# Seven products for the output projections of even blocks, and one whole turn for the reciprocals of the softmax sums

## The chip, the cores and the metric

One NeuronCore of one Trainium2 chip runs the whole kernel. The metric is the device time of one execution in microseconds (us). Engines are named as in the profile: PE is TensorE, DVE is VectorE, ACT is ScalarE, POOL is GpSimd, and SP is SyncE, whose queue issues almost all DMAs.

## The reference, cut to what matters

A transformer block with conditioned norms (adaLN), float32 throughout. B = 8 sequences of T = 1024 tokens, D = 512 channels, H = 16 heads of 32, hidden size HD = 2048:

```python
mod = silu(condition) @ Wada + bada                      # six rows of D per sequence
sh_a, sc_a, gt_a, sh_m, sc_m, gt_m = split(mod, 6, axis=1)
xm = layernorm(x, g1, be1) * (1 + sc_a) + sh_a
x = x + gt_a * (causal_attention(xm, Wqkv) @ Wproj + bproj)
xm = layernorm(x, g2, be2) * (1 + sc_m) + sh_m
x = x + gt_m * (gelu(xm @ W1 + b1) @ W2 + b2)
```

The change touches the product with Wproj, and the reciprocal of the row sums by which the softmax divides.

## The kernel before, in words

**Blocks.** The 8 x 1024 tokens are 16 blocks of 512 (`blocks`, L90): two halves per sequence. An even block n attends to its own 512 keys, an odd one to those and to the 512 of the block before it, so odd blocks have the longer attention. For each block the kernel computes k, q and v from the first norm, attends, projects the result with Wproj (`proj`), adds it to the residual, norms it a second time (key `m{n}`, steps `mt`), and runs the MLP: four `u` steps (up) and four `d` parts (down).

**Seven products.** Nearly every 512 x 512 x 512 product is made by a Strassen scheme (`strassen`, L896): quarters of 256, seven products instead of eight, each with a moving operand of 256 columns. `ORDER` (L304) lists the seven weight pieces. Sums of weight quarters (S1 to S4) are made once and kept in DRAM; sums of the activation's quarters (T1 to T4) are made anew each time by DVE and POOL. Three partial results stay in SBUF between the products: `p1`, `u2` and `u4`, one buffer each in the pool `tmp`. The last two products of a call go on as a side thread (`tail`, L975) while the main thread walks on; a later call that still finds the previous tail unfinished (`tail_key`) waits with `u2` for it (L960). The down parts `d` use the same three buffers: `u1` and `u3` in `p1`, `u5` in `u4`, `u2` in `u2` (L1364), and hold `u2` and `u5` from one part to the next.

**Output projections.** `by_quarters` (L292) chooses how block n is projected. Odd blocks 1 to 13 go through `project_quarters` (L1067), which calls `strassen` with `settled`, a function that gates each quarter of the result and adds it to the residual. The T sums live in the tiles of the second norm (`xm_m`, `t_m`), which are allocated early for that in `sums_of` (L1089). Blocks 0, the even ones and 15 go the direct way (`project_out`, L1131): four tiles of 128 tokens, each an accumulation over four pieces of Wproj with a moving operand of 512 columns, a DVE instruction that multiplies PSUM with the gate into `y` (L208), and one addition to the residual `xr` by POOL or DVE (L170 or L167, whichever `either` thinks will be done first).

**What sets the order.** The instruction order on each engine is written by the program itself. `plan` (L246) lists the linear steps of each window w; in window w the core attends block w, while the linear stream does the projection, second norm and MLP of block w - 1 and the k, q, v of block w + 1. A cost model (`now`, `written`, `left`, `note_*`) stands for each engine's clock; `work` advances the linear thread with the shortest wait, and `step_aside` and `pace` interleave it with attention units. In odd windows from w = 5 on the order is: d parts 1 and 2 of block w - 2, `proj` of the even block n = w - 1, `mt` of n, d part 3 of block w - 2, k and q of w + 1, then the `u` steps of n (L269). So `proj` of an even block stands between two d parts which share `u2` and `u4`.

**From the projection to the MLP.** After `proj` come row statistics (DVE L623, L624), the power for 1/sqrt (POOL L645 to L648), the normalized rows `hat_m` (L659, L664), their turn by 32 x 32 blocks (DVE L704) and through DRAM (DMAs L713, L718), the modulation (L775, L781) and the T sums (L791 to L796). Only then can the first `u` step run.

**Activation tiles.** `xm` and `t` have two buffers each and are handed out in turn: one to the first norms (`a{n}`), one to the second norms (`m{n}`), because allocations of the two kinds alternate.

**Weights.** Pieces of 256 KB go through a ring of 8 (`fetch`, L351) in a fixed order; a piece is loaded when the piece eight places ahead of it is released.

**Reciprocals.** `finish` (L1820) ends a head group g of block n. A matmul with ones gives the row sums, already repeated over 32 partitions; ACT copies them to `rec` and the numerator to `top`. `gather` turns a quarter of `rec` (128 columns) by 32 x 32 blocks into a small tile `squares` (L1850) and takes the reciprocals of the 4 columns that matter (L1852); there are four such jobs. `spread_out` (L1857) turns the 16 reciprocals back over 512 columns, and one multiplication makes the result in `qT` (L1885).

Matmuls on 128 x 32 tiles are issued four at a time, once per strip of 32 columns, and each float32 matmul stands in the trace as two instructions. So one call of `matmul` (L212) is 8 instructions; it is called a set below.

Of the kernel before, what the change touches and what calls it, by code (L numbers as in the profile page):

```python
# [22 lines left out]
def kernel(  # L23
# [268 lines left out]
    def by_quarters(n):  # L292
        return 0 < n < NB - 1 and (blocks[n][1])

# [192 lines left out]
    def norm_columns(name, shift_at, gain_at, o_g, o_b):  # L487

        gain = const.tile([P, NC, B], F32, tag=f"gain{name}", name=f"gain{name}")
        shift = const.tile([P, NC, B], F32, tag=f"shift{name}", name=f"shift{name}")  # L490
        one_plus = small.tile([P, NC, B], F32, tag="onep", name=f"onep{name}", bufs=1)
        nc.vector.tensor_scalar(one_plus, modT[:, ts(gain_at, NC), :], 1.0, None, ALU.add)
# [232 lines left out]
    def modulated(key, gain, shift, b, guards):  # L725
# [170 lines left out]
    def strassen(step, x, dest, target, row, done, settled=None):  # L896
# [52 lines left out]

        k1, k2, k4 = "p1", "u2", "u4"  # L950
        a = yield from product("A11", "B11")
# [33 lines left out]
        written[key] = NEVER  # L985
        tail_key[0] = key
        start(tail())
# [79 lines left out]
    def project_quarters(n):  # L1067
# [752 lines left out]
    def finish(n, g):  # L1820
# [24 lines left out]
        part = TB // 4  # L1845
        wide = TB // 4

        def gather(i):
            squares = small.tile([P, wide], F32, tag="squares", name=f"squares_{n}_{g}_{i}", bufs=1)
            nc.vector.transpose(squares, rec[:, ts(i, wide)])  # L1850
            some = inverse[:, ts(i, wide // Q)]
            nc.vector.reciprocal(some, squares.rearrange("p (a i) -> p a i", i=Q)[:, :, 0])  # L1852
            note("DVE", 160 + 1.05 * wide + 100, [kr], [kr])

        def spread_out(i=0, m=TB):
            some = inverse[:, i * m // Q : (i + 1) * m // Q].unsqueeze(2).to_broadcast([P, m // Q, Q])
            nc.vector.transpose(rec[:, ts(i, m)].rearrange("p (a i) -> p a i", i=Q), some)  # L1857
            note("DVE", 140 + 1.05 * m, [kr], [kr])

        inverse = small.tile([P, TB // Q], F32, tag="inverse", name=f"inverse_{n}_{g}", bufs=1)  # L1860
        if (n, g) == groups[-1]:
            for i in range(NTT):
                gather(i)
                spread_out(i, part)
# [5 lines left out]
        if (n, g) == first_end:  # L1870
            for i in range(4):
                gather(i)
            spread_out()
# [15 lines left out]

        for i in range(4):  # L1890
            add_job(lambda i=i: gather(i), [kr], g == NC - 1)
        add_job(quotient, [kr], g == NC - 1)
# [115 lines left out]
    for n in range(NB):  # L2008
# [80 lines left out]
```

## Time and profile before

| | us |
|---|---|
| median of 3 runs (lowest, highest) | 3508.98 (3507.87, 3513.93) |
| the profiled execution's own time | 3501.11 |
| its span, first to last instruction | 3499.4 |
| PE busy | 3441.3 |
| DVE busy | 2203.8 |
| POOL busy | 2113.7 |
| ACT busy | 1212.8 |

The profiled execution's own time is 1.7 us above its span. A share of busy time is an average over stages; the groups of instructions (by line, engine and shape) give the count, the busy time and the mean duration of one, and after the bar the idle time of that engine just before them. The clock that PE was granted was 0.998 of full speed over the span.

### The profile page before, as it was taken

How to read it: one execution, taken by the hardware profiler on the slowest of the kernel's cores; microseconds unless marked ns; L12 is line 12 of the kernel's file. 1: busy time of each engine (PE TensorE's matmuls, PEld its weight loads, DVE VectorE, ACT ScalarE, POOL GpSimd, SP SyncE). 2: the span in 40 equal slices, each digit the busy share in tenths (PEclk: the TensorE clock that was granted, in tenths of full speed). 3: DMA queues.
4: the chain of work that ended last, by engine and by line, in shares of the span. 5: the costliest groups of instructions: out<-in, count | busy, mean ns of one | idle time of the engine just before them, and what ended most of it. 6: DMA issues, size and time to landing. Idle time of an engine off the chain costs nothing. (4 is left out here: it accounts for less than half of the span.)

```text
span 3499.4 us, 122173 instructions
## 1 busy us (share of the span) xinstructions
PE 3441.3 (98%) x55101; PEld 1750.9 (50%) x55101; DVE 2203.8 (63%) x2808; ACT 1212.8 (35%) x1272; POOL 2113.7 (60%) x2255
## 2 busy tenths in 40 slices
PE   8999999999999999999999999999999999999999
PEld 4444455445544555445554455544555445554555
DVE  5775675565666566565666656665666656656573
ACT  2335333342343513335232442333423333323521
POOL 3667847667366663767627676375762857628640
PEclk9999999999999999999999999999999999999999
DMA  6763444535535455363554535545455454543344
GB/s 213 237 188 104 137 125 139 147 104 171 147 118 158 119 162 149 103 182 116 152 152 127 159 116 152 153 137 146 130 154 143 130 144 132 154 126 98 104 134 140
DMA packets 335580, 498.84 MB, mean 143 GB/s; under 512 B 27724, under 2 KB 184460, under 8 KB 331476
## 3 DMA queue, kind: packets, MB, share of 16 engines
q1 hardware_dynamic: 334944, 490.99, 47.8%
q8 instruction: 434, 7.11, 0.8%
q14 instruction: 86, 0.70, 0.1%
q10 hardware_dynamic: 116, 0.03, 0.0%
HBM read 432.13 MB, written 56.69 MB: 140 GB/s over the span
## 5 line engine op out<-in xcount | busy, mean ns | idle before, releaser
L1911 POOL TENSOR_TENSOR pT<-pT,pT 128x256 f32<-128x256 f32 (+3 forms) x1254 | 1224.7, 1012 | 238.9 <-PE po L1810 123.9
L1782 ACT ACTIVATE pT<-st 128x2048 f32<-128x2048 f32 x288 | 541.1, 1879 | 1017.5 <-PE st L1770 886.3
L217 PE MATMUL bank<-w,hT 128*32 128x256 f32 x14336 | 822.1, 380 | 0.0
L1694 DVE TENSOR_REDUCE mx<-sc 128x4 f32<-128x2048 f32 (+3 forms) x383 | 663.3, 1753 | 200.5 <-PE sc L1679 194.7
L217 PEld LDWEIGHTS bank<-w,hT 128*32 128x32 f32 x14336 | 448.0, 110 | 389.8 <-issue 109.7
L217 PE MATMUL bank<-xm_m,w 128*32 128x256 f32 x8192 | 497.4, 381 | 2.3 <-ACT p_u L197 1.0
L217 PE MATMUL bank<-t_m,w 128*32 128x256 f32 x6144 | 384.0, 380 | 2.5 <-DVE qT L208 1.4
L217 PEld LDWEIGHTS bank<-xm_m,w 128*32 128x32 f32 x8192 | 255.5, 110 | 227.3 <-issue 56.6
L1787 POOL TENSOR_SCALAR_AFFINE_SELECT pT<-pT 128x512 f32<-128x512 f32 x256 | 177.3, 710 | 313.7 <-ACT pT L1782 313.3
L1679 PE MATMUL sc<-kT,qT 32*128 32x512 f32 (+3 forms) x3064 | 328.0, 520 | 3.1 <-DVE mx L1694 1.8
L1691 DVE TENSOR_TENSOR sc<-sc,mask 128x1024 f32<-128x1024 f32 (+1 forms) x160 | 162.8, 1017 | 255.2 <-PE sc L1679 210.8
L1810 PE MATMUL po<-pT,v 128*32 128x512 f32 (+3 forms) x3048 | 301.7, 490 | 2.5 <-POOL pT L1787 2.3
L1770 PE MATMUL st<-qT,kT 32*128 32x512 f32 (+3 forms) x3072 | 302.7, 487 | 0.0
L217 PEld LDWEIGHTS bank<-t_m,w 128*32 128x32 f32 x6144 | 188.9, 110 | 178.8 <-issue 49.8
L217 PE MATMUL bank<-xm_a,w 128*32 128x256 f32 x3968 | 241.6, 380 | 2.4 <-ACT p_k L197 1.1
L1679 PEld LDWEIGHTS sc<-kT,qT 32*128 32x128 f32 x3064 | 129.2, 183 | 182.4 <-issue 82.4
L208 DVE TENSOR_TENSOR hT<-bank,u_u 128x512 f32<-128x512 f32 x186 | 126.0, 686 | 127.2 <-PE bank L217 126.5
L217 PE MATMUL bank<-t_a,w 128*32 128x256 f32 x2944 | 182.3, 380 | 1.4 <-ACT qT L204 0.9
L1885 POOL TENSOR_TENSOR qT<-top,rec 128x512 f32<-128x512 f32 x61 | 79.8, 1309 | 170.7 <-DVE rec L1857 167.8
L217 PE MATMUL bank<-w,qT 128*32 128x512 f32 (+1 forms) x1824 | 175.4, 515 | 3.7 <-DMA w<-in_L_cond_Wproj_dram 3.7
L1199 ACT ACTIVATE hT<-hT,cols 128x512 f32<-128x512 f32 x256 | 164.7, 711 | 40.7 <-DVE hT L208 27.4
L217 PEld LDWEIGHTS bank<-xm_a,w 128*32 128x32 f32 x3968 | 123.9, 110 | 101.3 <-issue 16.9
(262 smaller groups left out, 3657.1 us busy)
## 6 DMA issues: line engine op xcount, KB each, us to landing
w<-in_L_cond_W_dram SPq DMA_DIRECT2D x384, 256.0 KB
w<-kept_up_S SPq DMA_DIRECT2D x256, 256.0 KB
w<-kept_down_S SPq DMA_DIRECT2D x256, 256.0 KB
w<-kept_qkv_S SPq DMA_DIRECT2D x180, 256.0 KB
w<-in_L_cond_Wqkv_dram SPq DMA_DIRECT2D x147, 256.0 KB
hat_a<-in_x_dram SPq DMA_DIRECT2D x64, 256.0 KB
xr<-in_x_dram SPq DMA_DIRECT2D x32, 512.0 KB
out_dram<-xr SPq DMA_DIRECT2D x31, 512.0 KB
```

Of the source, the lines that this page charges most:

```text
L208: nc.vector.tensor_tensor(out, src, other, op)
L217: nc.tensor.matmul(ps[r, :], columns, rhs, start=start, stop=stop, skip_group_check=True)
L1199: nc.scalar.activation(hT[:, i, :], hT[:, i, :], AF.Gelu, bias=cols[:, O_B1 + f : O_B1 + f + 1])
L1679: nc.tensor.matmul(sc[:, j, c0 : c0 + w], qTs[n][r, gg, ts(qt, P)], keys_of(n, kh)[r, gg, :w], start=True, stop=True, skip_group_check=True,)
L1691: nc.vector.tensor_tensor(place, place, shape_of.to_broadcast(place.shape), ALU.add)
L1694: nc.vector.tensor_reduce(maxima[n, gg][:, kh, qt, :], sc[:, :, c0 : c0 + w], axis=AX.X, op=ALU.max)
L1770: nc.tensor.matmul(st[:, j, c0 : c0 + w], kT[r, gg, ts(k % NTT, P)], qT[r, gg, TB - w :], start=False, stop=True, skip_group_check=True,)
L1782: nc.scalar.activation(pT[:, :, :used], st[:, :, :used], AF.Exp, scale=scale)
L1787: nc.gpsimd.affine_select(diagonal, diagonal, pattern=[[0, HPG], [1, P]], compare_op=ALU.is_ge, fill=0.0, base=0, channel_multiplier=-1,)
L1810: nc.tensor.matmul(po[r, TB - w :], v[:, k % NTT, g * P + j * hd : g * P + (j + 1) * hd], pT[:, j, c0 : c0 + w], start=(k == 0), stop=last ...
L1885: nc.gpsimd.tensor_tensor(qTs[n][:, g, :], top, rec, ALU.mult)
L1911: nc.gpsimd.tensor_tensor(into, into, pT[:, j, c0 : c0 + w], ALU.add)
```

## The change

- `by_quarters` is true for all blocks 1 to 14, so the seven even blocks 2 to 14 go through `project_quarters` too. Blocks 0 and 15 stay direct.
- In a call with `settled`, for odd blocks too, the partial results `u2` and `u4` lie in the lower half of the second norm's tile `xm_m` (the upper half's left quarter is T1). Such a call no longer waits for the tail before it, and later calls do not wait for its tail.
- `sums_of` waits until the tile of the first norm of block n + 2 has been handed out (`placed`), so that the two buffers still alternate.
- `gather` turns all 512 columns of `rec` in place with one instruction and takes all 16 reciprocals with one; only the very last group still works in four parts. The tile `squares` goes. The model's costs for both turns are changed.
- `one_plus` of the norm columns gets two buffers; it is used twice in the whole kernel.

```diff
     def by_quarters(n):
-        return 0 < n < NB - 1 and (blocks[n][1])
+        return 0 < n < NB - 1
...
-        one_plus = small.tile([P, NC, B], F32, tag="onep", name=f"onep{name}", bufs=1)
+        one_plus = small.tile([P, NC, B], F32, tag="onep", name=f"onep{name}")
...
+        if key[0] == "a":
+            written["placed", int(key[1:])] = 0.0
...
         def partial(kind):
+            if settled is not None and kind != "p1":
+                return xm_of[x][kind]
             return tmp.tile([P, 2, HB], F32, tag=kind, name=f"{kind}_{name}", bufs=1)
...
-        k1, k2, k4 = "p1", "u2", "u4"
+        k1, k2, k4 = ("p1", "u2", "u4") if settled is None else ("p1", "own u2", "own u4")
...
-        if written.get(before, 0.0) == NEVER:
+        if settled is None and written.get(before, 0.0) == NEVER:
             yield [before], []
...
         written[key] = NEVER
-        tail_key[0] = key
+        if settled is None:
+            tail_key[0] = key
         start(tail())
...
         def sums_of():
-            yield [("v done", n + 1)], []
+            yield [("v done", n + 1), *([("placed", n + 2)] if n + 2 < NB else [])], []
...
             part["T1"] = xm[:, one, left_half]
+            part["u2"] = xm[:, two, left_half]
+            part["u4"] = xm[:, two, right_half]
...
-        def gather(i):
-            squares = small.tile([P, wide], F32, tag="squares", name=f"squares_{n}_{g}_{i}", bufs=1)
-            nc.vector.transpose(squares, rec[:, ts(i, wide)])
-            some = inverse[:, ts(i, wide // Q)]
-            nc.vector.reciprocal(some, squares.rearrange("p (a i) -> p a i", i=Q)[:, :, 0])
-            note("DVE", 160 + 1.05 * wide + 100, [kr], [kr])
+        def gather(i, m=TB):
+            nc.vector.transpose(rec[:, ts(i, m)], rec[:, ts(i, m)])
+            some = inverse[:, i * m // Q : (i + 1) * m // Q]
+            nc.vector.reciprocal(some, rec[:, ts(i, m)].rearrange("p (a i) -> p a i", i=Q)[:, :, 0])
+            note("DVE", 325 + 1.27 * m, [kr], [kr])
...
-            note("DVE", 140 + 1.05 * m, [kr], [kr])
+            note("DVE", 180 + 1.04 * m, [kr], [kr])
...
-        for i in range(4):
-            add_job(lambda i=i: gather(i), [kr], g == NC - 1)
+        add_job(lambda: gather(0), [kr], g == NC - 1)
...
         written["m used", n] = NEVER
+        written["placed", n] = NEVER
```

More of the change, by code (lines that the diff above doesn't have):

```diff
@@ L1845, in finish @@
         part = TB // 4
-        wide = TB // 4
-        def gather(i):
-            squares = small.tile([P, wide], F32, tag="squares", name=f"squares_{n}_{g}_{i}", bufs=1)
-            nc.vector.transpose(squares, rec[:, ts(i, wide)])
-            some = inverse[:, ts(i, wide // Q)]
-            nc.vector.reciprocal(some, squares.rearrange("p (a i) -> p a i", i=Q)[:, :, 0])
-            note("DVE", 160 + 1.05 * wide + 100, [kr], [kr])
+        def gather(i, m=TB):
[3 more added lines that the diff above has]
+            note("DVE", 325 + 1.27 * m, [kr], [kr])
         def spread_out(i=0, m=TB):
@@ L1862, in finish @@
             for i in range(NTT):
-                gather(i)
+                gather(i, part)
                 spread_out(i, part)
@@ L1870, in finish @@
         if (n, g) == first_end:
-            for i in range(4):
-                gather(i)
+            gather(0)
             spread_out()
@@ L1888, in quotient @@
                 written["attended", n] = 0.0
-        for i in range(4):
-            add_job(lambda i=i: gather(i), [kr], g == NC - 1)
+        add_job(lambda: gather(0), [kr], g == NC - 1)
         add_job(quotient, [kr], g == NC - 1)
```

## The prediction

> **What bounds the kernel now.** I read the page's busy times and slices first, then the waits of PE, then the seven stretches in which even blocks are projected.
>
> ```profile
> PE 3441.3 (98%) x55101; PEld 1750.9 (50%) x55101; DVE 2203.8 (63%) x2808; ACT 1212.8 (35%) x1272; POOL 2113.7 (60%) x2255
> PE   8999999999999999999999999999999999999999
> ```
>
> PE is busy 98% of the span, and nine tenths or more of every slice after the first. 3499.4 - 3441.3 = 58 us of idle time remain. The waits of PE (total, times, longest, in us) say who ended them:
>
> ```profile
> PE bank L449 <- ACT cond_act L443: 7.1, 1, 7.1
> PE st L1758 <- DVE mx L1694: 4.2, 6, 1.6
> PE bank L217 <- DMA w<-in_L_cond_Wproj_dram: 3.7, 4, 1.5
> ...
> PE bank L217 <- ACT xm_m L781: 1.4, 3, 0.7
> ```
>
> The largest is at the start. Nothing else is over 5 us in 3499, so no other engine, no DMA and no chain bounds more than a scrap of the time: what PE does not have to do is saved, and what makes PE wait is lost. The second norm's chain (ACT xm_m) costs 1.4 us over all sixteen blocks.
>
> The change acts in seven stretches, so these are read by themselves (each from the first projection matmul of blocks 2, 4, ... 14 to the last of its row statistics):
>
> ```profile
> core 0: us, PE busy (x) PEld busy (x) DVE busy (x) ACT busy (x) POOL busy (x), PEclk, DMA share, GB/s
> 623.00:655.00 32.00, 30.66 (x356) 11.02 (x360) 16.93 (x19) 5.42 (x5) 15.06 (x18) 1.00 0.35 113
> 1042.00:1077.00 35.00, 35.00 (x408) 12.49 (x401) 29.00 (x33) 10.36 (x10) 25.46 (x26) 1.00 0.51 147
> 1468.00:1499.00 31.00, 31.00 (x352) 10.99 (x344) 24.04 (x31) 7.11 (x6) 20.45 (x22) 1.00 0.43 126
> 1891.00:1925.00 34.00, 33.72 (x424) 12.68 (x416) 26.51 (x33) 7.37 (x7) 24.08 (x26) 1.00 0.42 126
> 2318.00:2345.00 27.00, 26.52 (x303) 8.89 (x299) 20.18 (x28) 7.37 (x7) 25.27 (x30) 1.00 0.47 128
> 2743.00:2772.00 29.00, 27.85 (x340) 10.19 (x332) 22.60 (x29) 8.11 (x5) 26.79 (x29) 1.00 0.23 73
> 3177.00:3209.00 32.00, 30.89 (x396) 11.96 (x388) 19.73 (x23) 7.99 (x5) 30.79 (x37) 1.00 0.27 83
> sum 220.00, PE 215.64 PEld 78.23 DVE 159.00 ACT 53.72 POOL 167.90; mean PE 30.81 PEld 11.18 DVE 22.71 ACT 7.67 POOL 23.99
> ```
>
> PE is full there too (215.6 of 220 us). But DVE is at 72% and POOL at 76%, and in the last three stretches POOL is at 94, 92 and 96%. That is where the change can hurt.
>
> **PE's own work.** Directly, a block takes 4 tiles x 4 pieces = 16 sets of 512 columns. By seven products it takes 7 x 4 = 28 sets of 256.
>
> ```profile
> 1894.14 2.78 PE L217 MATMUL bank<-w,qT 128*32 128x512 f32 x24
> 1896.74 0.41 PE L1732 MATMUL bank<-ident_b,mcols 128*32 128x128 bf16 x16
> ```
> ```profile
> L217 PE MATMUL bank<-w,qT 128*32 128x512 f32 x128 | 14.1, 592 | 0.0
> ```
> ```profile
> 3397.73 97.74 PE bank L217 x1792
> ```
>
> The first pair is from block 8: 24 instructions, three sets, and the next work starts 2.60 us later, so 0.867 us a set and 16 x 0.867 = 13.9 us. The second row, block 15 alone on PE, has 16 sets in 14.1 us. The third, from the chain, is the MLP of the last block: 1792 instructions are 224 sets in 97.74 us, 0.436 each, so 28 cost 12.2 us. The saving is 13.9 - 12.2 = 1.7 us a block (1.9 by the other row), 7 x 1.7 = **11.9 us**. The attention units between the sets stay the same in number, so I count no more changes from one kind of matmul to another.
>
> **Work that is added for DVE and POOL.** Odd blocks already do this, so their rows give the prices:
>
> ```profile
> L208 DVE TENSOR_TENSOR u_proj<-bank,p_proj 128x512 f32<-128x512 f32 x7 | 4.8, 679 | 0.0
> L1097 DVE TENSOR_TENSOR xm_m<-qT 128x512 f32<-128x512 f32 x7 | 6.8, 975 | 0.0
> L167 DVE TENSOR_TENSOR y<-y,row_ga 128x512 f32<-128x512 f32 x8 | 9.5, 1184 | 0.3
> ```
> ```profile
> L170 POOL TENSOR_TENSOR y<-y,row_ga 128x512 f32<-128x512 f32 x13 | 16.6, 1275 | 20.8 <-DVE y L208 20.8
> L170 POOL TENSOR_TENSOR t_m<-t_m,qT 128x512 f32<-128x512 f32 x7 | 12.1, 1728 | 36.4 <-PE po L1810 29.6 <-DVE t_m L1097 6.8
> ```
>
> Both kinds have four evacuations into `y` and four additions. New are: the copy of `p1` (DVE or ACT), `u2` and `u4` (2 x 0.68 on DVE), T1 (0.98) and three more sums (two on DVE at some 0.69, T3 on POOL 1.73), and three gate multiplications, 8 of 21 on DVE (1.18) and 13 on POOL (1.28). Per block that is 0.35 + 1.36 + 0.98 + 1.38 + 1.35 = 5.4 us on DVE and 1.73 + 2.4 = 4.1 us on POOL. In the stretches of blocks 2 to 8, DVE and POOL have room for it beside PE. In those of blocks 10, 12 and 14 they are busy 45.5 of 54, 49.4 of 58 and 50.5 of 64 us together; 9.5 more fill the first two. What is late then is the attention's accumulation of pT on POOL and its maxima on DVE, or the norm's chain. PE has d part 3, k and q to do instead, so I put half a us of idle time on each of these three blocks, and none on the others; bounds 0 and 3 us each.
>
> [...]
>
> ```profile
> L167 DVE TENSOR_TENSOR xr<-xr,y 128x512 f32<-128x512 f32 x21 | 22.3, 1062 | 0.9
> L1171 DVE TENSOR_TENSOR xr<-xr,y 128x512 f32<-128x512 f32 x4 | 2.8, 692 | 0.1
> ```
>
> The same addition takes 1062 ns amid POOL's work and 692 ns in the tail. The prices above were measured amid it, so most of this is in them; beside a POOL that is 94% busy instead of 76 it would be more. [...]
>
> **The norm's chain.** In the direct way three of the four tiles are finished before the last, and only one statistic comes behind the last addition. With seven products both halves of the rows are finished by the last two deliveries, each of which needs a gate multiplication more, and two to four statistics (0.67 + 0.18 = 0.85 us each) follow where it is one now:
>
> ```profile
> L623 DVE BATCH_NORM_STATS2 st_m<-xr 128x6 f32<-128x512 f32 x60 | 40.1, 669 | 0.0
> ...
> L624 DVE BATCH_NORM_AGGREGATE mv_m<-st_m 128x2 f32<-128x6 f32 x60 | 10.9, 182 | 2.1
> ```
>
> So the chain leaves the last matmul later by about 1.3 + 1 to 3 x 0.85 = 2.1 to 3.9 us, and that matmul comes 1.7 us earlier: 0.4 to 2.2 us net. How tight it is shows in block 8:
>
> ```profile
> 1961.24 2.93 ACT L781 ACTIVATE xm_m<-hat_m,shiftm,gainm 128x512 f32<-128x512 f32 x4 [5.23 <-DMA hat_m<-held_m]
> ...
> 1966.31 1.27 POOL L170 TENSOR_TENSOR t_m<-t_m,xm_m 128x512 f32<-128x512 f32 x1
> ...
> 1967.83 1.48 PE L217 MATMUL bank<-xm_m,w 128*32 128x256 f32 x24
> ```
>
> The first `u` matmul starts at 1967.83 and the last T sum ends at 1967.58; modulated tiles are ready from 1964.2. So there are up to 3 us of slack at the first product, and the later T sums are wanted only some products on. In odd blocks, which already have the long chain, PE's whole wait for it is the 1.4 us above. I take 0.1 us a block; bounds 0 and the full 2.2.
>
> **The gathers.** Each of 63 groups (all but the last) does four turns and four reciprocals now:
>
> ```profile
> 705.27 0.30 DVE L1850 STREAM_TRANSPOSE squares<-rec 128x128 f32<-128x128 f32 x1
> ...
> 707.50 0.71 DVE L1857 STREAM_TRANSPOSE rec<-inverse 128x512 f32<-128x512 f32 x1
> ```
> ```profile
> L1852 DVE RECIPROCAL inverse<-squares 128x4 f32<-128x4 f32 x256 | 45.7, 178 | 8.8
> ```
>
> The four pairs last 707.50 - 705.27 = 2.23 us. Afterwards there are one turn of 512 columns (0.71 by the row of the turn back) and one reciprocal of 16 columns, between 178 and 4 x 178 = 712 ns; I take 0.3, near the short end, since a reciprocal of 4 columns must be mostly fixed cost. Saved: 2.23 - 1.0 = 1.2 us, or 63 x 1.2 = 76 us of DVE in all. DVE is not the bound; it is worth at most PE's 4.2 us of waits for maxima, and the four groups of a window save nearly what the projection adds on DVE, though only one of them falls near it. I take 1 us gained; bounds 0 and 4. That the turn is now one job which can hold a maximum up for 1.0 instead of 0.5 us I cost at nothing, since four such jobs usually ran in a row, as here.
>
> **Weights and order.** Three more pieces of 256 KB a block are 5.4 MB of 499; the DMA share in the seven stretches is 0.23 to 0.51. In SP's queue they come one at a time as products release them, as for odd blocks. Wproj pieces made PE wait 3.7 us in all, in both kinds of block; I take no change, bounds 2 us either way. The new wait on `placed` delays nothing if the tile of block n + 2's first norm is handed out before the projection begins. Its step stands one d part earlier, and its rows were normed a whole window part before, so I cost it at nothing; behind it would queue T1 and thus the third product, while `d` and attention go on.
>
> **Sum.** -11.9 (PE) + 1.5 (late blocks) + 0.7 (chain) - 1 (gathers) = -10.7 us; with some rounding against me for a new order of everything, **-10 us**. The profiled execution took 3501.11 us, 1.7 more than its span, so this would be 3491. The median of the runs shown is 7.9 us above it; from there, 3508.98 - 10 = **3499 us**.
>
> **Rivals.** (1) *The engines beside PE take most of it back.* If each projection costs PE 1 to 2 us in waits, for the chain or for POOL's and DVE's backlog, 7 to 14 of the 11.9 us are lost: 3504 to 3511, about 3506. For it: POOL at 92 to 96% in three stretches. Against it: odd blocks do all this with PE at 203.6 of 205 us in their stretches:
>
> ```profile
> sum 205.00, PE 203.62 PEld 110.40 DVE 146.14 ACT 51.42 POOL 127.72; mean PE 33.94 PEld 18.40 DVE 24.36 ACT 8.57 POOL 21.29
> ```
>
> But POOL is at 62% there. (2) *Slower.* The written order has PE stand at a matmul whose operand is late. If the backlog puts off the end of the chain by the whole 3.9 us at each of the seven blocks and PE stands still for it, 7 x 3.9 = 27 us are lost, 15 net: 3524. It becomes a loss from 1.7 us of standing a block, 2.7 for one that is measured. For it: the slack in block 8 is under 3 us. Against it: the model that writes the order knows the chain, and lets attention go first. (3) *More than forecast.* Shorter gathers bring the maxima forward and PE's waits for DVE and for weights nearly vanish: 4 + 4 us more, 3491. (4) *The seven products don't save*: only if a set of 256 cost over 0.495 us (13.9 / 28); no row has that.
>
> **Chances.** Forecast (3494 to 3502) 0.48; rival 1 0.25; rival 2 0.14; rival 3 0.13; rival 4 none. A measurement of this kernel tells apart about 0.2%, 7 us. Faster by more (below 3502): 0.60. Within it: 0.26. Slower by more: 0.14. The range takes in rivals 1 and 3 and the near part of 2: 3488 to 3515.
>
> **What would show it.** Right: the groups with `w,qT` keep 128x512 for two blocks only (256 instructions instead of 1152), PE's busy time falls by some 12 us while its idle time stays within 5 us, the four turns of a group have become one of 512 columns at about 0.7 us, and the first `u` matmul follows its T sums without a gap. Wrong: idle time of PE ahead of `xm_m`, `po` or `sc` matmuls in the seven stretches, released by ACT xm_m, POOL pT or DVE mx; POOL near 100% in them; or PE busy time that does not fall because the sets are cut into shorter runs.

## The result, and the profile after

The changed kernel takes 3540.30 us (median of 5 runs, 3538.51 to 3543.59) against 3507.87 us (5 runs, 3502.97 to 3513.93) before: a ratio of 1.0102, 95% interval 1.0092 to 1.0113 (the two medians alone give 1.0092). It is slower by 1%; 3499 us was predicted. The profiled execution took 3541.93 us, with a span of 3540.2.

The busy times of after:

```profile
PE 3445.6 (97%) x55773; PEld 1775.2 (50%) x55773; DVE 2193.2 (62%) x2477; ACT 1216.1 (34%) x1284; POOL 2163.5 (61%) x2278
```

The span grew by 40.8 us. (By the medians it is 32.4 us: the profiled execution of before, with 3501.11 us, was quicker than its median.) PE is busy 4.3 us more, though it has less to do, and idle for 94.6 us where it was 58.1. The largest of its waits (total, times, longest, in us):

```profile
PE bank L217 <- DVE t_m L1104: 9.8, 5, 3.0
PE st L1765 <- DVE mx L1701: 6.5, 9, 2.4
...
PE bank L1739 <- POOL mcols L1723: 6.0, 3, 2.6
PE po L1817 <- POOL pT L1794: 5.1, 4, 2.1
```

The first line is not among the waits of before: products of a projection wait for their T sums. (Lines of after stand 7 further down: L1701 is L1694 of before, L1104 is L1097.) Next, the seven stretches of the even projections, the last three and the sum of all:

```profile
2350.00:2379.00 29.00, 26.45 (x460) 14.16 (x452) 26.34 (x25) 7.98 (x7) 27.88 (x24) 1.00 0.37 110
2771.00:2801.00 30.00, 26.18 (x401) 12.60 (x396) 23.50 (x24) 9.03 (x10) 26.93 (x19) 1.00 0.54 161
3215.00:3247.00 32.00, 30.19 (x472) 15.52 (x476) 24.02 (x27) 7.36 (x6) 30.75 (x27) 0.95 0.31 92
sum 223.00, PE 206.33 PEld 104.52 DVE 177.06 ACT 59.89 POOL 198.35; mean PE 29.48 PEld 14.93 DVE 25.29 ACT 8.56 POOL 28.34
```

PE has 206.3 of 223 us there, so 16.7 us idle instead of 4.4; DVE went from 72% to 79%, POOL from 76% to 89%. But much of the loss lies outside these stretches. The first projection product of blocks 2 and 8 starts, before and then after, at:

```profile
623.77 1.49 PE L217 MATMUL bank<-w,qT 128*32 128x512 f32 x12 [1.54 <-DMA w<-in_L_cond_Wproj_dram]
...
1891.92 1.04 PE L217 MATMUL bank<-w,qT 128*32 128x512 f32 x8
```
```profile
646.05 1.93 PE L217 MATMUL bank<-w,qT 128*32 128x256 f32 x32 [0.56 <-DMA w<-in_L_cond_Wproj_dram]
...
1919.54 1.05 PE L217 MATMUL bank<-w,qT 128*32 128x256 f32 x16
```

**22 of the 40.8 us are lost before the first even projection begins**, 5 between it and block 8, and 13 behind that. So there are at least two causes.

**The sum in the trace's own terms.** The time adds up with a quantity that the prediction left out, the granted clock. Here are two windows of the run *even_only* (below) behind waits of PE: us, busy time of each engine, then PEclk.

```profile
2757.03:2763.86 6.83, 2.77 (x28) 1.38 (x32) 6.25 (x11) 0.00 (x0) 4.80 (x5) 0.50 0.01 2
1941.25:1944.66 3.41, 3.41 (x28) 1.16 (x28) 0.90 (x1) 2.45 (x4) 3.41 (x4) 0.50 0.82 308
```

After these waits the clock is halved for 6.83 and 3.41 us. A matmul then takes about twice its time, and counts as busy: eight `st` matmuls on 512 columns (L1777) take 1.96 us at 1941.42 and 1.03 at 1933.46, at full clock. Summed over the trace's clock records, half-clock time was 13.2 us before and is 47.9 after. At most half of that difference, 17.3 us, is PE time lost with PE "busy". Take it off and PE's busy time changed by 4.3 - 17.3 = -13.0 us (-11.9 predicted). In part PE was idle in those stretches: it was busy for 10.2 us of them before and for 41.2 after, which makes 15.5 us lost and -11.2 of work. So +36.5 idle, some +15.5 through the half clock and some -11.2 of work make up the +40.8. That the last of these comes out near the saving that was worked out from the sets supports the split. The same for each run, with half of all half-clock time taken off:

| kernel | median us | ratio (95% interval) | span against before | idle | half-clock us | PE busy at full clock |
|---|---|---|---|---|---|---|
| after | 3540.30 | 1.0102 (1.0092, 1.0113) | +40.8 | +36.5 | +34.7 | -13.0 |
| even_only | 3529.60 | 1.0071 (1.0056, 1.0086) | +27.3 | +25.5 | +28.0 | -12.2 |
| own_tile_odd | 3510.44 | 1.0003 (0.9991, 1.0014) | +2.7 | +2.2 | -0.3 | +0.6 |
| gather_only | 3524.87 | 1.0064 (1.0047, 1.0081) | +23.0 | +16.5 | +16.8 | -1.9 |
| model_only | 3506.25 | 1.0006 (0.9997, 1.0016) | +4.1 | +2.7 | +3.0 | -0.1 |
| whole_old_order | 3504.08 | 0.9991 (0.9982, 1.0000) | +0.6 | -1.2 | +3.3 | +0.2 |
| small_new_order | 3530.57 | 1.0071 (1.0052, 1.0091) | +23.4 | +19.5 | +13.3 | -2.7 |
| pool_light_before | 3487.13 | 0.9953 (0.9934, 0.9971) | -16.8 | -10.9 | +0.6 | -6.2 |
| pool_light_even | 3487.12 | 0.9944 (0.9930, 0.9959) | -12.6 | +3.0 | +10.4 | -20.8 |
| late_quotients | 3522.93 | 1.0049 (1.0034, 1.0064) | +23.6 | +12.3 | +20.6 | +1.0 |
| even_late_sums | 3543.32 | 1.0097 (1.0080, 1.0114) | +44.6 | +31.1 | +52.1 | -12.6 |
| even_late_sums_defer | 3541.45 | 1.0104 (1.0089, 1.0119) | +38.5 | +31.1 | +34.5 | -9.9 |
| even_defer_whole | 3539.74 | 1.0098 (1.0083, 1.0113) | +43.9 | +30.5 | +42.1 | -7.6 |
| even_at_early | 3556.47 | 1.0145 (1.0130, 1.0160) | +55.2 | +45.0 | +51.3 | -15.4 |
| before_at_early | 3502.42 | 0.9985 (0.9975, 0.9994) | +3.6 | +2.0 | +13.8 | -5.3 |
| even_whole_old | 3529.62 | 1.0070 (1.0051, 1.0088) | +22.0 | +24.0 | +20.5 | -12.2 |
| even_at_early_whole | 3550.26 | 1.0129 (1.0112, 1.0146) | +44.6 | +39.6 | +38.7 | -14.3 |
| even_2_to_6 | 3495.75 | 0.9970 (0.9959, 0.9982) | -0.9 | +0.2 | +13.1 | -7.7 |
| at_early_whole | 3501.04 | 0.9984 (0.9974, 0.9993) | -2.1 | -2.3 | +7.4 | -3.5 |

Each ratio is against runs of before on the same chip. The four last columns are of the profiled executions, us against the profiled execution of before; "idle" is span less PE's busy time, the last is busy time less half of the half-clock time (it overstates a gain where a half-clock stretch is itself partly idle). Kernels with the same PE work as before stand between -6.2 and +1.0 in it, so it is good to some 6 us. Profiled executions of one kernel differ by some us, and that of before was a quick one, which puts the span column some 5 to 7 us too high for a run whose profile lies near its median. So a few us in these columns decide nothing; the ratios do.

### The profile page after: what moved, and what is told of

It is laid out like the page before. It is cut to its first block, busy times and chain, and to the rows that moved or that the text cites. A ratio compares the mean times of both kernels' runs of the same rounds, so it can differ in the third digit from the quotient of the medians.

```text
span 3540.2 us, 123351 instructions
## 1 busy us (share of the span) xinstructions
PE 3445.6 (97%) x55773; PEld 1775.2 (50%) x55773; DVE 2193.2 (62%) x2477; ACT 1216.1 (34%) x1284; POOL 2163.5 (61%) x2278
## 5 line engine op out<-in xcount | busy, mean ns | idle before, releaser
L1701 DVE TENSOR_REDUCE mx<-sc 128x4 f32<-128x2048 f32 (+3 forms) x383 | 663.5, 1753 | 222.8 <-PE sc L1686 216.5
L1777 PE MATMUL st<-qT,kT 32*128 32x512 f32 (+3 forms) x3072 | 302.4, 489 | 0.0
L1777 PEld LDWEIGHTS st<-qT,kT 32*128 32x128 f32 x3072 | 144.6, 187 | 25.5 <-issue 0.8
```

Of the source, the lines that this page charges most:

```text
L1701: nc.vector.tensor_reduce(maxima[n, gg][:, kh, qt, :], sc[:, :, c0 : c0 + w], axis=AX.X, op=ALU.max)
L1777: nc.tensor.matmul(st[:, j, c0 : c0 + w], kT[r, gg, ts(k % NTT, P)], qT[r, gg, TB - w :], start=False, stop=True, skip_group_check=True,)
```

## The experiments

### The two halves of the change

*even_only* keeps the even projections, their own tile and `placed`, with the old gathers. *own_tile_odd* is the same with the direct way back for even blocks. *gather_only* is the kernel before with the whole gather and its new model costs. *model_only* changes one cost of the model.

```diff
# even_only: the diff of the change without gather, spread_out and one_plus
# own_tile_odd, against even_only
-        return 0 < n < NB - 1
+        return 0 < n < NB - 1 and (blocks[n][1])
# model_only, against before
-            note("DVE", 140 + 1.05 * m, [kr], [kr])
+            note("DVE", 180 + 1.04 * m, [kr], [kr])
```

> The changed kernel's projections, partial results and wait, with the four small gathers of the kernel before. Theory A: slower like the changed kernel, 3530 to 3540. Rival B: the saving of 12 us on PE appears, about 3500.

> Odd blocks alone by seven products as before, but with u2 and u4 in the norm's tile, without the waits for tails and with the wait on placed; small gathers. Theory A: same as before within 5 us. Rival C (the loss comes from letting the tails of odd blocks run free of the next call): slower by 10 to 25 us.

> The kernel before with the whole turn in place and one reciprocal per group (and the two cost lines of the model that go with it), projections untouched. Theory A (the time is lost at the new projections of even blocks, where DVE cannot deliver the T sums in time): same as before within 5 us, about 3506. Rival B (the new costs of the turns rewrite the order of every engine from block 0 on, and the new order has more places where PE stands still): slower by 15 to 30 us, about 3530, with PE's idle time up already before 500 us of the span.

> The kernel before with one number of its cost model changed (the turn back is taken as 712 ns instead of 678); the same instructions, in whatever order the model then writes. Theory A: same within 5 us. Rival B: the order alone moves the time by 10 us or more, mostly upward, with the same instructions.

Both halves lose: 0.71% for the projections, and 0.64% for the gathers, whose loss was no rival of the prediction. They do not add up: 1.35% together, where the whole change shows 1.02%. The own tile costs nothing, and neither does no longer waiting for the tail: the instruction order of *own_tile_odd* is that of before. *model_only* told nothing, since its order came out as before too.

### The gathers: the instruction or the order

The model's costs decide the written order on every engine, so a cheaper job can change all of it. *whole_old_order* does the whole turn in place, but notes it in the model as the four old jobs; the order of every engine but DVE's own gathers is then that of before. *small_new_order* is the reverse: four small turns as one job, noted at the whole turn's cost; PE, ACT, POOL and SP have the order of *gather_only*.

```diff
# whole_old_order, against before
 def gather(i):
-            squares = small.tile([P, wide], F32, tag="squares", name=f"squares_{n}_{g}_{i}", bufs=1)
-            nc.vector.transpose(squares, rec[:, ts(i, wide)])
-            some = inverse[:, ts(i, wide // Q)]
-            nc.vector.reciprocal(some, squares.rearrange("p (a i) -> p a i", i=Q)[:, :, 0])
+            whole = (n, g) != groups[-1]
+            if i == 0 or not whole:
+                m = TB if whole else wide
+                nc.vector.transpose(rec[:, ts(i, m)], rec[:, ts(i, m)])
+                some = inverse[:, i * m // Q : (i + 1) * m // Q]
+                nc.vector.reciprocal(some, rec[:, ts(i, m)].rearrange("p (a i) -> p a i", i=Q)[:, :, 0])
             note("DVE", 160 + 1.05 * wide + 100, [kr], [kr])
```

> The whole turn in place with one reciprocal, but noted in the cost model like the four small gathers, so that every other instruction stands in the order of the kernel before on all engines. Theory B (the loss of gather_only is the order that the new cost writes): same as before within 5 us, 3500 to 3510, or a few us faster. Rival (the long turn itself holds DVE up, or costs more than four short ones): 3520 to 3530 as gather_only.

> The other half of that pair: four small gathers as before, but as one job with the cost of the whole one, so that PE, ACT, POOL and SP have the order of gather_only. Theory B: 3520 to 3535, like gather_only or a little slower. Rival: 3507 as before.

The instruction is innocent: with the old order the whole turn is as fast or a little faster (0.9991), and with the new order the four old turns lose as much (1.0071) as the whole one (1.0064). The loss has a place, too. The busy times from 400 to 500 us, in *whole_old_order*, *gather_only*, *small_new_order* and after, in this order (us, then PE, PEld, DVE, ACT, POOL):

```profile
400.00:500.00 100.00, 99.44 (x1580) 50.37 (x1575) 69.59 (x78) 32.68 (x34) 65.83 (x91) 1.00 0.43 125
```
```profile
400.00:500.00 100.00, 87.71 (x1374) 44.37 (x1367) 60.33 (x74) 32.23 (x31) 72.03 (x90) 0.97 0.34 103
```
```profile
400.00:500.00 100.00, 90.15 (x1424) 45.93 (x1420) 66.19 (x95) 33.33 (x32) 71.45 (x91) 0.98 0.32 99
```
```profile
400.00:500.00 100.00, 88.36 (x1369) 44.09 (x1362) 58.32 (x73) 33.30 (x34) 68.93 (x87) 0.95 0.36 113
```

PE stands for 10 to 12 us in each of the three with the new order, around the projection of block 1, and for 0.6 us with the old one; most of what else is lost by block 2 is lost between 100 and 400 us. One of these waits in the timeline of after, on PE, DVE and POOL (start, us, ..., idle time before and what ended it); it stands with the same 2.50 us in *gather_only*:

```profile
454.57 0.64 PE L217 MATMUL bank<-w,t_m 128*32 128x256 f32 x8 [2.50 <-DVE t_m L1104]
```
```profile
453.42 1.10 DVE L1104 TENSOR_TENSOR t_m<-qT,xm_m 128x512 f32<-128x512 f32 x1 [5.67 <-POOL qT L1889]
```
```profile
446.20 5.96 POOL L1914 TENSOR_TENSOR pT<-pT,pT 128x384 f32<-128x384 f32 x8
452.13 1.25 POOL L1889 TENSOR_TENSOR qT<-top,rec 128x512 f32<-128x512 f32 x1
```

The quotient of the last head group, which the T sums need, stands on POOL behind eight additions of the attention (5.96 us). DVE is idle for 5.67 us meanwhile, and then PE for 2.50. But the place of the quotient is not what changed. In the kernel before, POOL and then PE at the same point:

```profile
425.97 5.55 POOL L1911 TENSOR_TENSOR pT<-pT,pT 128x384 f32<-128x384 f32 x8
...
432.67 1.27 POOL L1885 TENSOR_TENSOR qT<-top,rec 128x512 f32<-128x512 f32 x1
```
```profile
436.81 1.91 PE L217 MATMUL bank<-w,qT 128*32 128x256 f32 x32
438.54 1.04 PE L1831 MATMUL bank<-pT,ones 128*32 128x512 f32 x8
439.51 1.15 PE L1679 MATMUL sc<-kT,qT 32*128 32x384 f32 x16
440.59 1.93 PE L217 MATMUL bank<-w,t_m 128*32 128x256 f32 x32
```

The quotient follows the same eight additions there. What differs is PE's order: before, attention instructions stand between the first product of the projection and the one that needs a T sum, and one more attention unit (`st` and `po`) ahead of the first; in *gather_only* and in after there is nothing in between (450.14, 1.93 us, then the wait). The new order asks for the sum before it can be there.

*late_quotients* measures what a late quotient costs by itself: in the kernel before, POOL writes the last quotient of blocks 2 to 14 (even) four times instead of once, some 3.8 us later at seven places, the order unchanged.

```diff
-                nc.gpsimd.tensor_tensor(qTs[n][:, g, :], top, rec, ALU.mult)
+                late = 4 if g == NC - 1 and n > 0 and n % 2 == 0 else 1
+                for _ in range(late):
+                    nc.gpsimd.tensor_tensor(qTs[n][:, g, :], top, rec, ALU.mult)
```

> The kernel before, in its order, in which POOL writes the last quotient of the even blocks 2 to 14 four times over (the same values), so that the direct projection gets its operand some 3.9 us later. It measures what a stall of PE costs. Clock theory (a stall of 2 us or more makes the clock fall to half for 3.4 us or more): up to 7 x (2 to 4) us of idle time and up to 7 stretches at half clock, the time rising by the idle time and half of the stretches. Without it: the time rises by the idle time alone.

7 x 3 x 1.25 = 26 us of POOL work cost 16 us by the medians (3522.93 against 3506.98), and 23.6 between the two profiled spans: 12.3 us of idle time, and 20.6 more at half clock. So about half of the delay shows as standing of PE, and the clock adds to it. The wait that grew most is the one for the next work of POOL (`mcols`, 8.7 us against 2.4).

### The even projections: backlog or order

Two theories remained for the 0.71%: the engines beside PE are too full in these stretches (D), or the order puts the projection's products too early, ahead of sums that cannot be ready (E). *pool_light_before* and *pool_light_even* leave out the additions of pT for two of the four heads of each group (`j` counts heads), so the row sums of these heads lack all units of key tiles but the first; the additions stay noted in the model, so the order of everything else is unchanged.

```diff
-                    nc.gpsimd.tensor_tensor(into, into, pT[:, j, c0 : c0 + w], ALU.add)
+                    if j % 2 == 0:
+                        nc.gpsimd.tensor_tensor(into, into, pT[:, j, c0 : c0 + w], ALU.add)
```

> The kernel before, leaving out two of the four pT accumulations of each key tile on POOL (the softmax sums of two heads in four are wrong; about 600 us of POOL work less), noted in the cost model as if they were there, so the order stays. It is the partner of pool_light_even. Theory D (POOL's and DVE's backlog at the projections is what makes PE stand still): 3490 to 3505, since before has little of that.

> even_only with the same half of the pT accumulations left out and the order of even_only. Theory D: PE's idle time in the seven stretches falls from 21 us to under 8, the clock stays up, and the saving of 12 us shows: 5 to 12 us faster than pool_light_before, about 3490. Rival E (the written order of the new projections is at fault whatever the load: T sums right behind the first product): still 10 us or more slower than pool_light_before.

Their busy times, in this order:

```profile
PE 3435.4 (99%) x55101; PEld 1747.8 (50%) x55101; DVE 2109.9 (61%) x2808; ACT 1211.4 (35%) x1272; POOL 1501.1 (43%) x1635
```
```profile
PE 3425.7 (98%) x55773; PEld 1769.1 (51%) x55773; DVE 2154.9 (62%) x2847; ACT 1218.2 (35%) x1288; POOL 1562.8 (45%) x1668
```

With POOL at 43 to 45%, the deficit of 23 us is gone: 3487.13 against 3487.12. So the load of POOL, with what it does to DVE, is needed for most of it. But the even projections should then have gained 11.9 us; PE's busy time is indeed 9.7 us lower, and its idle time is 14 us higher (61.1 against 47.2). By the starts of the projections in the two traces, *pool_light_even* is 7.9 us ahead of its partner at block 10 (2302.9 against 2310.8) and loses 12 us behind it. The order, or DVE, has a share that this pair does not take away. The pair also relieves POOL everywhere, not in the seven stretches alone, so it does not tell by which way the load acts.

*even_late_sums* tries E's remedy: in even blocks the products whose operands need only one sum come first. *even_late_sums_defer* also puts the addition of d part 2 and its settling in among POOL's jobs, so that they do not stand ahead of the T sums on DVE; *even_defer_whole* adds the whole turn at its old cost.

```diff
# even_late_sums, against even_only
+        early = early or (settled is not None and step[1] % 2 == 0)
# even_late_sums_defer, against even_late_sums
-            add_to(v3, u2, [key("u2")], [key("v3")])
-            settle(n, 0, 1, v3, key("v3"))
+            if n % 2 and 1 < n < NB - 1:
+                pool_jobs.insert(0, (add_up, [key("u2"), kv]))
+            else:
+                add_up()
```

> even_only with one thing changed: at even blocks the product A12 x B21, which needs no T sum, goes ahead of S2 x T2, so DVE has two products' time (3.4 us instead of 1.7) for T1 and T2. Theory D+E (a backlog on DVE and POOL meets an order that wants the T sums 1.7 us after the first product): the 6.7 us of waits for the T sums nearly vanish and with them half-clock stretches; 5 to 12 us faster than even_only, about 3518 to 3524. Theory D alone (the backlog moves on to the maxima and the accumulations): within 4 us of even_only.

> The same, and the three additions and multiplications with which d part 2 settles its quarter are issued within the projection instead of just ahead of its T sums, on DVE or POOL. Theory D+E: the T sums start some 4 us earlier; 5 us faster again, about 3512. Theory D alone: no gain, since the same work is only moved by a few us.

> The same again, with the whole turn in place noted at the old cost (whole_old_order), so that the order stays and DVE has 1.2 us less a group. Theory D: DVE's relief takes some of the waits for maxima; 3 to 8 us faster than even_late_sums_defer. If it comes below 3500 it beats both kernels.

All three are slower than *even_only* (1.0097 to 1.0104). The waits for T sums fell, and others took their place; here *even_only* and then *even_late_sums*:

```profile
PE st L1765 <- DVE mx L1701: 8.7, 8, 2.8
...
PE bank L217 <- DVE t_m L1104: 6.7, 4, 2.3
```
```profile
PE st L1766 <- DVE mx L1702: 13.9, 10, 2.8
...
PE bank L217 <- DVE t_m L1105: 3.7, 2, 2.3
```

The waits for T sums went down by 3.0 us and those for maxima up by 5.2. The same DVE has to make both. The longest wait of *even_only* but for the one at the start shows why that queue matters. PE and then DVE at block 12:

```profile
2761.09 3.27 PE L217 MATMUL bank<-w,qT 128*32 128x256 f32 x32 [5.67 <-DVE mx L1673]
```
```profile
2752.97 1.66 DVE L167 TENSOR_TENSOR v_d<-v_d,u_d 128x512 f32<-128x512 f32 x1
2754.66 1.65 DVE L167 TENSOR_TENSOR v_d<-v_d,row_gm 128x512 f32<-128x512 f32 x1
2756.41 1.56 DVE L167 TENSOR_TENSOR xr<-xr,v_d 128x512 f32<-128x512 f32 x1
2757.90 0.68 DVE L1104 TENSOR_TENSOR xm_m<-qT 128x512 f32<-128x512 f32 x1
2758.68 0.69 DVE L1104 TENSOR_TENSOR t_m<-qT,xm_m 128x512 f32<-128x512 f32 x1
2759.41 0.69 DVE L167 TENSOR_TENSOR t_m<-qT,t_m 128x512 f32<-128x512 f32 x1
...
2760.34 0.69 DVE L1673 TENSOR_REDUCE mx<-bank 128x1 f32<-128x512 f32 x1
```

DVE works nearly without a gap: the end of d part 2 (three instructions of 1.6 us), three T sums, then the mask and the first maximum, with whose end the projection's product starts. From 2752.97 on no instruction on DVE begins late; too much of it stands ahead of what PE wants. The window of half clock from 2757.03 to 2763.86, shown with the result, lies over the end of this wait.

### Does the linear stream run dry before k?

In *even_only*, 7.0 us pass at block 8 between the last product of d part 3 and the first of k of block 10; in the kernel before it is at most 1.1 us at any block. k needs the first norm of that block, whose turns (L704) stand on DVE behind the projection's own work. *even_at_early* lists that norm's step one d part earlier, *before_at_early* is its control, and *even_at_early_whole* and *even_whole_old* have the whole turn at its old cost, with and without the move.

```diff
-                late = m[5:6] + at + m[6:]
+                late = at + m[5:]
```

> The even projections alone (old gathers), with one step of the plan moved: the first norm of block n + 2, which k of block n + 2 needs, is listed ahead of d part 1 instead of behind it. Theory G (the linear stream runs dry between d part 3 and k, because the turns of that first norm stand on DVE behind the projection's own work): the 7.0 us between the last product of d part 3 and the first of k at block 8 fall to about 1, the idle time falls by 5 us or more from 79.4, and the ratio lies between 0.999 and 1.004. Theory D (backlog of POOL and DVE through the stretches): the work is the same, the stalls come elsewhere, ratio 1.005 to 1.009 as without the move.

> The control: the kernel before with the same step moved. Both theories: in the kernel before k starts at most 1.1 us behind d part 3, so nothing is to be gained; 0.999 to 1.002, with idle time between 50 and 60 us. A gain here of over 0.3% would mean that the move is good for another reason than the projections.

> The even projections and the whole turn in place, but the turn noted in the model with the four costs of before: the change without its new costs. Theory O (the gather's loss is the order written from its new cost, in block 1): the stretch from 100 to 500 us is as before (idle 400 to 500 us about 1 us instead of 12), and the time is that of the even projections alone, 1.005 to 1.009. Rival (the whole turn itself holds maxima up once POOL and DVE are fuller): 1.009 to 1.012 as the full change.

> Both mends: the first norm's step moved ahead, and the whole turn noted at the old costs. Theory G with O: 0.997 to 1.002, the 11.9 us of the PE saving partly kept. Theory D: 1.004 to 1.009.

The theory fell. The pause at block 8 shrank from 7.0 to 2.3 us, and the kernel became slower (1.0145): its waits rose elsewhere. A second pause of this kind, 8.4 us ahead of a v at 2996.6, hardly changed (7.7).

```profile
PE st L1765 <- DVE mx L1701: 16.0, 14, 3.1
PE bank L217 <- DVE t_m L1104: 11.0, 4, 5.1
```

In the kernel before the same move gains a little (0.9985). *even_whole_old* settles the other question: with the old costs, the whole turn adds nothing to the loss of *even_only* (3529.62 against 3529.60), so the 10.7 us between *even_only* and the full change are the order from the new costs as well.

### Where the even projections lose

By the starts of the projections in the trace, *even_only* is level with before until block 8 and loses 28 us behind it:

```profile
1891.15 1.48 PE L217 MATMUL bank<-w,qT 128*32 128x256 f32 x24
```

1891.15 here, 1891.92 before; the spans are 3526.7 and 3499.4. *even_2_to_6* therefore keeps seven products for blocks 2, 4 and 6 only. *at_early_whole* combines, without even projections, the two edits that had lost nothing.

```diff
# even_2_to_6, against even_only
-        return 0 < n < NB - 1
+        return 0 < n < NB - 1 and (blocks[n][1] or n < 8)
```

> Seven products for blocks 2, 4 and 6 only (old gathers), the blocks in whose stretches POOL is busy for 47 to 73% before; blocks 8 to 14 stay direct. By the starts of the projections, the kernel with all seven stands 0.8 us ahead of the kernel before when block 8 is projected (1891.1 against 1891.9) and loses 28 us behind that. Theory D (backlog; what a projection costs goes with how full POOL and DVE are there): all of the loss is in the blocks that stay direct now, so 0.998 to 1.001, and PE's busy time falls by some 5 us. Rival (any change of the work puts the written order off, wherever it stands): a loss of 10 us or more all the same, 1.003 or above, with stalls behind block 8 too.

> The two edits that lost nothing, in the kernel before, without the even projections: the whole turn in place noted at the old four costs, and the first norm's step listed ahead of d part 1 in windows of even blocks. If their gains (0.9991 and 0.9985, each hardly more than its interval) are real and add up: 0.996 to 0.999. If they are the scatter of one order against another: 0.998 to 1.001.

*even_2_to_6* beats both kernels: 3495.75 us, ratio 0.9970 (0.9959 to 0.9982), with 6 runs against 16 of before.

```profile
span 3498.5 us, 122849 instructions
```

Seven products in blocks 8, 10, 12 and 14 thus cost 3529.60 - 3495.75 = 34 us together, 8.5 on average, where 1.7 each was to be saved; with blocks 2, 4 and 6 alone the kernel gains. The order of the instructions behind block 8 is not that of before in *even_2_to_6* either, so a changed order alone is not what loses. That the load at the place decides fits blocks 10 to 14, with POOL at 92 to 96% before; it was not shown block by block, and it does not tell block 8 (POOL 71%, DVE 78% in its stretch before) from block 4 (73% and 83%). The profiled execution was the slowest of the six and shows a gain of 0.9 us only, so how the gain of the median (12 us, 6 to 14 by the interval) divides into the 5.1 us of three projections and the rest was not settled. An order alone can move this kernel by 0.15% (*before_at_early*), so some of it may be luck. *at_early_whole* (0.9984) is no faster than *before_at_early* alone (0.9985): the two small gains do not add up.

## Why the prediction was wrong, point by point

**PE's own work: right.** 28 sets of 256 columns replaced 16 of 512. PE's busy time at full clock fell by 12.2 us in *even_only* and 13.0 in after, or by 9.6 and 11.2 if only the busy part of the half-clock stretches is counted; 11.9 was predicted. The groups of after:

```profile
L217 PE MATMUL bank<-w,qT 128*32 128x512 f32 x256 | 28.8, 593 | 0.0
...
L217 PE MATMUL bank<-w,qT 128*32 128x256 f32 x1344 | 84.7, 384 | 2.9 <-DMA w<-in_L_cond_Wproj_dram 2.0 <-ACT xm_m L204 0.9
...
L217 PE MATMUL bank<-w,t_m 128*32 128x256 f32 x1344 | 86.2, 390 | 10.5 <-DVE t_m L1104 9.8 <-DVE y L208 0.6
```

**"PE has d part 3, k and q to do instead, so I put half a us of idle time on each of these three blocks": this step failed.** The list of what is late named the right things (maxima, pT) but not the T sums, and the products that wait for them stand in PE's written order ahead of d part 3. In place of 1.5 us, *even_only* shows 25.5 us more idle time and 11 to 14 us through the half clock. The bounds of 0 and 3 us a block came from nothing in the trace, and the half clock stands nowhere in the sum. Block 8, which was to cost nothing, lost as well, with POOL at 71% in its stretch before: *even_only* is 0.8 us ahead of before at its projection and 6.8 behind at that of block 10 (2325.8 against 2319.0).

**The added work was mis-sized.** Predicted were 5.4 us of DVE and 4.1 of POOL a block. *even_only* against before has 47.6 us more on DVE and 59.1 on POOL: 6.8 and 8.4 a block. POOL got more of it than was counted, as `either` moves work over when DVE is full, and the instructions themselves became longer. In *even_only*:

```profile
L167 DVE TENSOR_TENSOR xr<-xr,y_d 128x512 f32<-128x512 f32 x15 | 28.2, 1881 | 1.0
...
L1104 DVE TENSOR_TENSOR xm_m<-qT 128x512 f32<-128x512 f32 x14 | 16.5, 1181 | 0.0
L1104 DVE TENSOR_TENSOR t_m<-qT,xm_m 128x512 f32<-128x512 f32 x14 | 12.9, 919 | 5.7 <-POOL qT L1892 4.7
```

Before, the second took 975 ns, the third 692 and the first 1169. The prediction said that such instructions would take longer beside a fuller POOL, and took most of that to be in its prices. In the seven stretches POOL is busy for 187.6 of 227 us (83%) in *even_only*, where it was 76% before; over its whole trace the sums of the third row took a third longer on average, and the additions of the first row 61%. Singly it shows in the sums of the third row: before, all seven took 691 to 693 ns, with nothing running on POOL, so POOL was not in that price; in after, nine took 691 to 693 ns (eight of them with POOL idle) and five 825 to 1572, each with POOL at work for at least 95% of its time. With POOL relieved (*pool_light_even*) DVE's total fell by 96 us, from 2251.4 to 2154.9, with the same instructions; not every group gained, the third row rose to 1003 ns.

**The gathers: the instruction right, the step wrong.** One turn in place took 699 ns and the reciprocal of 16 columns 254, together 0.95 us where 1.0 was assumed:

```profile
L1855 DVE STREAM_TRANSPOSE rec<-rec 128x512 f32<-128x512 f32 x63 | 44.1, 699 | 57.8 <-ACT rec L1847 57.7
...
L1857 DVE RECIPROCAL inverse<-rec 128x16 f32<-128x16 f32 x63 | 16.0, 254 | 2.2
```

**"with some rounding against me for a new order of everything" is the second step that failed.** It stood at 0.7 us; *gather_only*, *small_new_order* and *whole_old_order* together show that the order written from the new cost lost 0.64% by itself (23.0 us of span, with 18.8 of them behind by the projection of block 2, which starts at 642.6 us in *gather_only*). The prediction looked at the seven stretches only, though the gather is in all 64 groups.

**What a stall costs.** All of the prediction's prices for standing counted the stall's own length. The half clock behind it added almost half as much again (+36.5 idle, some +15.5 through the clock).

**The norm's chain, the weights, `placed`: as costed, or too small to see.** In after ACT xm_m ends 0.9 us of PE's waits (1.4 before), Wproj pieces 2.0 (3.7 before), and *own_tile_odd* with the new tile and `placed` has a ratio of 1.0003 (0.9991 to 1.0014).

**The rivals.** Rival 2 had the sign and the form (PE stands at a matmul whose operand is late) at the wrong place: not at the end of the norm's chain but at the start of the projection. Rival 1 named the backlog, at 7 to 14 us; *even_only* lost some 35 (23 by the medians, and the 12 that were to be saved). Rival 4, that nothing would be saved on PE, is refuted by the first point. The prediction's own sign of failure, idle time in the seven stretches released by pT or mx, did come (16.7 us instead of 4.4), but as the smaller part.

What stays open: why moving work (*even_late_sums*, *even_at_early*) loses 14 to 27 us more in the even projections, and how much of the 14 us of idle time in the pool_light pair is DVE and how much the order.

## What to carry to other kernels

Where a program writes its own instruction order from a cost model, an edit of a cost is an edit of every queue: price it by running the new instruction at the old costs, and the old one at the new costs. In a kernel whose bound engine is 98% busy, work taken from it is worth its length only where the engines that feed it have room at that very place; look at those engines' share stretch by stretch, and try the change on the stretches that have it (blocks 2 to 6 here: 0.9970; all: 1.0071). Count a stall of PE at its length, and what the clock does behind it besides: here 3.41 us at half clock or more followed each time PE had stood for 2.0 us or more of one window of 3.413 us (below).

## What the hardware showed

**Half clock came behind waits of 2 to 3 us, in kernels whose PE is 97 to 99% busy.** In *even_only* the first wait below was followed by 3.41 us at 0.50 (the window shown with the result), the second, longer one by none:

```profile
1941.13 0.55 PE L1765 MATMUL st<-mrow,minus_ones 32*128 32x512 bf16 x4 [2.41 <-DVE mx L1701]
```
```profile
1471.75 0.41 PE L1739 MATMUL bank<-ident_b,mcols 128*32 128x128 bf16 x16 [3.11 <-POOL mcols L1723]
```

So it was not the length alone. In each of the 20 traces the half-clock stretches begin whole multiples of 3.413 us apart: 952 and 30 of them in before, 9, 4, 60, 11, 26 and so on in after. Cut the time into windows of that length which begin where those stretches do, and the first wait lies in one window, while the second lies across two:

```profile
1937.84:1941.25 3.41, 1.00 (x12) 0.26 (x12) 2.29 (x1) 0.00 (x0) 3.33 (x5) 1.00 1.07 245
```
```profile
1466.80:1470.21 3.41, 1.84 (x35) 0.92 (x32) 3.31 (x3) 1.98 (x2) 3.33 (x4) 1.00 0.54 176
1470.21:1473.62 3.41, 1.87 (x40) 0.95 (x44) 1.61 (x3) 0.96 (x2) 3.19 (x5) 1.00 0.12 47
```

PE stands for 2.41 us of the first window, and for 1.57 and 1.54 us of the other two. Over all 20 traces, from 120 us on and without the last 5 us, there are some 19,650 such windows at full clock. All 100 of them in which PE stood for 2.0 us or more were followed by one at half clock, 20 of the 116 with 1.4 to 2.0 us, and none with less. In before alone these are 2 of 2 and none of 3, in after 7 of 7 and 3 of 11. No window had to be idle throughout: in after the 7 had PE standing for 2.09 to 2.88 of their 3.413 us.

**A reciprocal of few columns is mostly fixed cost:** 178 ns for 4 columns, 254 for 16 (the rows of L1852 before and L1857 after), so 12 more columns add 76 ns. **A turn of 512 columns in place** takes 699 ns, as long as the one from another tile (0.71 us).
